# Half sums in the other order, and two of three images combined near the end: a convolution kernel on one Trainium2 core

## The chip, the cores and the metric

The kernel runs on one core of a Trainium2 chip. The metric is the device time of one execution in microseconds (us), as the median of several executions. Each execution has a state, fast or slow; on this one core slow means over 1.5% above the fastest run of the same kernel. Profiles are of one execution each. Engines are named as in the profile: PE is TensorE's matmul, PEld its weight load, DVE VectorE, ACT ScalarE, POOL GpSimd, SP SyncE. "Step i" is the loop's turn that convolves image i.

## The reference

160 images of 128 channels and 32 x 32 pixels are group-normalised (32 groups of 4 channels), convolved 3 x 3 with weights that are first quantised in two stages, and added to themselves. Five weight sets take the images in turn.

```python
# cut: helper functions, the setup of the inputs
s1 = (beta - alpha) / 3.0;  v1 = s1 * floor(U / s1)          # beta, alpha: max and min of U
s2 = s1 / 5.0;              v2 = s2 * floor((U - v1) / s2)
w = (v1 + v2).reshape(OUT_CH * N, IN_CH, 3, 3)
act = conv_general_dilated(gn(x) as (32, 640, 32, 32), w, padding 1, feature_group_count=5)
return x + act
```

## The kernel before

The arithmetic that the argument needs: rows are convolved in pairs, so that each image needs two *half sums* m1 and m2 in PSUM (128 x 512 float32, one bank each), from which the accumulators of the even and odd rows start: m1 + m2 and m1 - m2. Every operand is split into a high and a low float16 part. A *plain* image multiplies its high part directly; a *combined* image (the odd ones from image 7 on) has row combinations `v` formed by DVE before the split, which saves PE some products and costs DVE more work.

```python
LOAD_LEAD = 20
...
self.xpool = pool("x", 12)          # pairs of images
self.zpool = pool("z", 3)
self.parts = pool("parts", 5)
self.rows = pool("rows", 4)         # low parts
self.wide = pool("wide", 1)         # v of combined images
self.wide_parts = pool("wide_parts", 2)   # their high parts
self.evac = pool("evac", 2)         # copies of m2
self.sums = pool("sums", 4)
...
def combined(self, i):
    return self.STEADY <= i < self.imgs and i % 2 == 1
...
def sums_of_pairs(self, i):         # PE: the half sums of image i
    m = self.m[i] = self.banks(self.ps_m, "m", i)       # ONE tile of two banks, pool of 1
    both = self.both(i)
    for a, kind in enumerate((self.SUM, self.DIFF)):    # m1, then m2
        for col in self.COLS:
            for j, (_, st) in enumerate(both):
                self.product(m[:, a], i, kind, st[:, a], col, ...)
...
def leave(self, i):                 # ACT: copy m2 out of PSUM
    m2 = self.evac.tile(...)
    self.nc.scalar.copy(m2, self.m[i][:, 1])
    ...
def pairs(self, i, between=lambda: None):   # DVE: the two pair operations
    ...
    nc.vector.tensor_add(rows[:, :, 0], m[:, 0], m2)
    between()
    nc.vector.tensor_sub(rows[:, :, 1], m[:, 0], m2)
```

In step i PE first does the half sums of image i+1, then the rest of image i. DVE does, in this order, the low part of i+2, the pairs of i+1, and `v` of i+4 where that is combined. SP issues all large transfers in one order: at the end of step i the store of the pair of images that is finished, then the load of a later pair, and now and then a set of weights:

```python
self.store(i - 2)
while loaded * NB < min(self.imgs, i + self.LOAD_LEAD):
    self.load(loaded)
    loaded += 1
```

The sum of an image with its convolution goes ACT (`sum` from PSUM), POOL (a DMA that adds `sum` to the x tile), SP (store). Then the x tile can be loaded again.

## Time and profile before

| | before |
|---|---|
| time, median of 3 (range) | 1001.79 us (1001.14 to 1002.22) |
| profiled span | 1000.1 us |
| first half-sum product of image 145 | 900.79 us |
| start of the last product | 992.78 us |
| between the two: "the tail" | 91.99 us |

The two stretches have different limits: up to about 905 us ACT is nearly as busy as PE, afterwards ACT has room. So the table cuts the run at image 145, and the two marks are taken from the matmul starts. The lines of the page that bound the kernel are shown and read in the prediction.

The columns are start, duration, engine, line and operation.

### The profile page before, as it was taken

The numbers are of one execution on the slowest core, as the hardware profiler recorded it, in microseconds if no ns is written. First come the engines' busy times: TensorE is split into PE (matmuls) and PEld (weight loads), VectorE is DVE, ScalarE is ACT, GpSimd is POOL, SyncE is SP. The second block draws the span as 40 slices with busy tenths as digits, with TensorE's granted clock in tenths as the row PEclk, the third lists the DMA queues.
The fourth block names the chain that finished last, engine by engine and source line by source line (L and its number), as shares of the span: only waits on it lengthen the run. The fifth ranks groups of instructions, "written<-read, shape, count | busy, mean of one in ns | idle before, by whom it ended". The sixth has DMA issues, their size and how long they took to land.

```text
span 1000.1 us, 15977 instructions
## 1 busy us (share of the span) xinstructions
PE 962.5 (96%) x5935; PEld 575.1 (58%) x5935; DVE 895.6 (90%) x1237; ACT 913.2 (91%) x1243; POOL 405.3 (41%) x575
## 2 busy tenths in 40 slices
PE   1999999999999999999999999999999999999997
PEld 0445555565655565666655566666565666666554
DVE  7999999998999999989999998999999988888884
ACT  4879999999999999999999999999999999998560
POOL 3435473553425262524364443426353523233310
PEclk9999999999999999999999999999999999999999
DMA  9628989999999999999989999999999999988773
GB/s 357 247 89 229 257 221 279 269 268 267 272 273 269 266 258 273 288 274 269 264 243 288 270 265 278 277 273 249 266 272 270 279 262 275 274 230 219 177 179 141
DMA packets 67287, 254.42 MB, mean 254 GB/s; under 512 B 5248, under 2 KB 5248, under 8 KB 67200
## 3 DMA queue, kind: packets, MB, share of 16 engines
q1 hardware_dynamic: 45168, 173.09, 50.2%
q0 software_dynamic: 22032, 80.23, 41.4%
q8 instruction: 48, 0.79, 0.3%
q14 instruction: 39, 0.32, 0.1%
HBM read 89.19 MB, written 83.89 MB: 173 GB/s over the span
## 4 chain that ended last, share of the span: by engine, by line
PE 73%; DVE 10%; ACT 10%; issue 3%; POOL 3%; DMA 1%; SPq 0%; DVEq 0%; POOLq 0%
PE eo L613 25%; PE m L651 25%; PE eo L651 22%; ACT junk L199 2%; ACT vh L560 2%; ACT sum L735 1%; ACT m L709 1%; DVE eo L719 1%; DVE eo L721 1%; ACT z L510 1%; ACT junk L192 1%; DVE lo L573 1%; DVE vl L566 1%; DMA range<-in_L_conv_U_dram 1%; DVE ext L421 1%
## 5 line engine op out<-in xcount | busy, mean ns | idle before, releaser
L651 PEld LDWEIGHTS <-wt 128*128 128x128 f16 x4212 | 409.0, 98 | 241.3 <-DVE eo L721 12.9
L613 PE MATMUL eo<-hi,wt 128*128 128x496 f16 (+1 forms) x1476 | 352.5, 375 | 1.1 <-ACT wt L475 0.6
L748 POOL DMA_DIRECT2D xt<-sum x153 | 136.5, 895 | 419.4 <-ACT sum L735 403.5
L613 PEld LDWEIGHTS <-wt 128*128 128x128 f16 x1548 | 151.3, 99 | 147.4 <-ACT wt L475 1.8
L566 DVE SCALAR_TENSOR_TENSOR vl<-v,rstd,vh 128x2048 f16<-128x2048 f32 x77 | 180.8, 2348 | 4.2 <-ACT vh L560 4.2
L651 PE MATMUL m<-vh,wt 128*128 128x496 f16 (+1 forms) x462 | 175.7, 380 | 5.2 <-DVE eo L721 4.6
L719 DVE TENSOR_TENSOR eo<-m,m 128x512 f32<-128x512 f32 x157 | 109.0, 695 | 77.8 <-ACT m L709 77.8
L651 PE MATMUL eo<-vl,wt 128*128 128x256 f16 (+1 forms) x924 | 177.1, 273 | 0.0
L651 PE MATMUL eo<-vh,wt 128*128 128x256 f16 (+1 forms) x924 | 177.1, 273 | 0.0
L651 PE MATMUL m<-vl,wt 128*128 128x496 f16 (+1 forms) x462 | 175.4, 380 | 0.0
L199 ACT ACTIVATE junk<-xt,mv 128x1024 f16<-128x1024 f32 x152 | 174.0, 1145 | 0.2
L192 ACT ACTIVATE junk<-xt 128x1024 f16<-128x1024 f32 x152 | 160.6, 1057 | 14.7 <-DMA xt<-in_x_dram 11.6
L735 ACT ACTIVATE sum<-eo 128x1024 f32<-128x1024 f32 x153 | 154.1, 1007 | 13.7 <-PE eo L651 13.7
L560 ACT ACTIVATE vh<-v,rstd 128x2048 f16<-128x2048 f32 x77 | 155.0, 2013 | 1.8 <-POOL v L539 1.8
L651 PE MATMUL eo<-rows,wt 128*128 128x248 f16 (+1 forms) x960 | 144.3, 273 | 0.0
L651 PE MATMUL m<-rows,wt 128*128 128x496 f16 (+1 forms) x480 | 116.9, 380 | 0.5 <-DVE eo L721 0.5
L709 ACT COPY m<-m 128x512 f32<-128x512 f32 x157 | 91.3, 582 | 27.4 <-PE m L651 23.9
L721 DVE TENSOR_TENSOR eo<-m,m 128x512 f32<-128x512 f32 x157 | 108.4, 691 | 1.0
L510 ACT ACTIVATE z<-xt,shift,rstd 128x1024 f32<-128x1024 f32 x83 | 103.2, 1243 | 3.5 <-POOL shift L242 3.5
L573 DVE TENSOR_TENSOR lo<-z,hi 128x1024 f16<-128x1024 f32 x83 | 101.5, 1223 | 0.0
L518 ACT CAST hi<-z 128x1024 f16<-128x1024 f32 x83 | 86.8, 1046 | 2.6
L549 DVE TENSOR_TENSOR v<-xt 128x960 f32<-128x960 f32 x77 | 88.4, 1149 | 0.0
(111 smaller groups left out, 863.3 us busy)
## 6 DMA issues: line engine op xcount, KB each, us to landing
xt<-in_x_dram SPq DMA_DIRECT2D x78, 1024.0 KB, 9.0
out_dram<-xt SPq DMA_DIRECT2D x78, 1024.0 KB, 5.2
xt<-sum POOLq DMA_DIRECT2D x153, 512.0 KB, 6.9
range<-in_L_conv_U_dram SPq DMA_DIRECT2D x4, 576.0 KB, 7.9
u<-in_L_conv_U_dram SPq DMA_DIRECT2D x4, 576.0 KB, 11.8
xt<-in_x_dram SPq DMA_DIRECT2D x4, 512.0 KB, 10.6
out_dram<-xt SPq DMA_DIRECT2D x3, 512.0 KB, 2.7
u<-in_L_conv_U_dram SPq DMA_DIRECT2D x2, 288.0 KB, 3.0
```

Source lines behind the costliest of these rows:

```text
L192: self.nc.scalar.activation(junk, image, ACTF.Copy, scale=-1.0 / image.shape[1], accum_out=self.mv[:, j, 0:1],)
L199: self.nc.scalar.activation(junk, image, ACTF.Square, bias=self.mv[:, j, 0:1], accum_out=self.mv[:, j, 1:2],)
L510: nc.scalar.activation(z, self.image(i), ACTF.Identity, bias=st.shift[:, j : j + 1], scale=st.rstd[:, j : j + 1],)
L560: self.nc.scalar.mul(vh, self.v[i], st.rstd[:, j])
L566: self.nc.vector.scalar_tensor_tensor(vl, self.v[i], st.rstd[:, j], self.hi[i], ALU.mult, ALU.subtract)
L573: self.nc.vector.tensor_sub(lo[:, 1 : self.H + 1, :].rearrange("p h w -> p (h w)"), self.z.pop(i), self.hi[i].rearrange("p h w -> p (h w)"),)
L613: nc.tensor.matmul(target[:, h, r0 - h0 : r1 - h0, c0:c1], self.wts[n, col][:, k, :], tile[:, s0 : s0 + r1 - r0, c0 + dw : c1 + dw], start ...
L651: self.nc.tensor.matmul(target[:, :, c0:c1], self.wts[n, col][:, kind, :], source[:, :, c0 + dw : c1 + dw], start=start, stop=stop, skip_g ...
L719: nc.vector.tensor_add(rows[:, :, 0], m[:, 0], m2)
L721: nc.vector.tensor_sub(rows[:, :, 1], m[:, 0], m2)
L735: nc.scalar.mul(self.sum[i], eo, 0.5)
L748: self.nc.gpsimd.dma_start(self.image(i), self.sum.pop(i), accum_op=ALU.add)
```

## The change

The intent has two parts. With m2 multiplied first, ACT could copy it while PE still does m1, and PE could start the next m2 as soon as that copy is done. And near the end, where ACT has room, two of three images are combined rather than one of two, which takes work from PE; for that `v` and its high part need more tiles, which are taken from x, `sum` and the lead of the loads.

```diff
-    LOAD_LEAD = 20
+    LOAD_LEAD = 18
+    THIRDS = 146
...
-        self.xpool = pool("x", 12)
+        self.xpool = pool("x", 11)
-        self.wide = pool("wide", 1)
-        self.wide_parts = pool("wide_parts", 2)
+        self.wide = pool("wide", 2)
+        self.wide_parts = pool("wide_parts", 3)
-        self.sums = pool("sums", 4)
+        self.sums = pool("sums", 3)
...
+        self.pair = self.ps_m.tile([P, 2, self.H // 2, self.W], F32, tag="m", name="m")
...
-        return self.STEADY <= i < self.imgs and i % 2 == 1
+        if i < self.STEADY or i >= self.imgs:
+            return False
+        return i % 2 == 1 if i < self.THIRDS else i % 3 != 1
...
-        m = self.m[i] = self.banks(self.ps_m, "m", i)
+        m = self.pair
-        for a, kind in enumerate((self.SUM, self.DIFF)):
+        for a, kind in ((1, self.DIFF), (0, self.SUM)):
...
-        self.nc.scalar.copy(m2, self.m[i][:, 1])
+        self.nc.scalar.copy(m2, self.pair[:, 1])
```

(Cut: the same renaming in the warm-up, in the first images and in `pairs`.)

More of the change, by code (lines that the diff above doesn't have):

```diff
@@ L377, in __init__ @@
         self.steps = Steps(nc, keep)
-        self.chunks, self.z, self.hi, self.v, self.eo, self.m = {}, {}, {}, {}, {}, {}
+        self.pair = self.ps_m.tile([P, 2, self.H // 2, self.W], F32, tag="m", name="m")
+        self.chunks, self.z, self.hi, self.v, self.eo, self.m2 = {}, {}, {}, {}, {}, {}
         self.sum = {}
@@ L620, in taps, with bank_pair @@
                 )
-    def banks(self, pool, tag, i):
-        return pool.tile([self.P, 2, self.H // 2, self.W], F32, tag=tag, name=f"{tag}{i}")
+    def bank_pair(self, i):
+        return self.ps_eo.tile([self.P, 2, self.H // 2, self.W], F32, tag="eo", name=f"eo{i}")
     def warm_up(self, count):
         zeros = self.los[3].rearrange("p h w -> p (h w)")
-        if "warm" not in self.m:
-            self.m["warm"] = self.banks(self.ps_m, "m", "warm")
         for _ in range(count):
             self.nc.tensor.matmul(
-                self.m["warm"][:, 0].rearrange("p i w -> p (i w)"), zeros[:, :128],
+                self.pair[:, 0].rearrange("p i w -> p (i w)"), zeros[:, :128],
                 zeros[:, :512], start=True, stop=True,
@@ L639, in direct_hi @@
         if i not in self.eo:
-            self.eo[i] = self.banks(*((self.ps_eo, "eo") if i < 2 else (self.ps_m, "m")), i)
+            self.eo[i] = self.bank_pair(i) if i < 2 else self.pair
         self.taps(i, (self.hi[i], 0), col, self.eo[i], False)
@@ L708, in leave @@
         m2 = self.evac.tile([self.P, self.H // 2, self.W], F32, tag="m2", name=f"m2_{i}")
-        self.nc.scalar.copy(m2, self.m[i][:, 1])
-        self.m[i] = self.m[i], m2
+        self.nc.scalar.copy(m2, self.pair[:, 1])
+        self.m2[i] = m2
     def pairs(self, i, between=lambda: None):
         nc = self.nc
-        m, m2 = self.m.pop(i)
-        eo = self.eo[i] = self.banks(self.ps_eo, "eo", i)
+        m1, m2 = self.pair[:, 0], self.m2.pop(i)
+        eo = self.eo[i] = self.bank_pair(i)
         rows = eo.rearrange("p h (i a) w -> p (h i) a w", a=2)
-        nc.vector.tensor_add(rows[:, :, 0], m[:, 0], m2)
+        nc.vector.tensor_add(rows[:, :, 0], m1, m2)
         between()
-        nc.vector.tensor_sub(rows[:, :, 1], m[:, 0], m2)
+        nc.vector.tensor_sub(rows[:, :, 1], m1, m2)
     def by_hand(self, i):
```

## The prediction

> **What bounds the kernel now.** I read the page first, then busy time in windows, then the list of waits, then timelines of single engines near the end of the run, and last the built program, in which each wait names the instruction that ends it.
>
> ```profile
> PE 962.5 (96%) x5935; PEld 575.1 (58%) x5935; DVE 895.6 (90%) x1237; ACT 913.2 (91%) x1243; POOL 405.3 (41%) x575
> ...
> L719 DVE TENSOR_TENSOR eo<-m,m 128x512 f32<-128x512 f32 x157 | 109.0, 695 | 77.8 <-ACT m L709 77.8
> ```
>
> ```profile
> 600.00:700.00 100.00, 99.92 (x631) 60.81 (x629) 90.51 (x121) 98.74 (x136) 41.73 (x60) 1.00 0.98 269
> 940.00:960.00 20.00, 20.00 (x131) 12.58 (x129) 16.10 (x21) 12.63 (x13) 3.79 (x7) 1.00 0.75 196
> ```
>
> ```profile
> PE m L651 <- DVE eo L721: 4.6, 9, 1.2
> ```
>
> The windows' columns are the engines' busy us in the order of the page, then clock, DMA share and GB/s. PE is the bound, at full clock. But ACT is at 98.7% too until it stops measuring images (image 159 is measured while 145 is convolved, near 905 us), so in the middle it can't catch up what it loses. Afterwards ACT falls to 63% and DVE is at 80%. The waits view (100 to 900 us) shows PE waiting only 4.6 us for DVE; as ends of matmuls are modelled, I also took starts: over the run, 32 first half-sum products come late against the pitch, by 10.5 us together. That is all that a better order could ever win.
>
> Matmul starts give the size of each image: a product of 512 columns every 0.216 us, one of 256 every 0.109.
>
> ```profile
> 920.29 1.46 PE L651 MATMUL m<-rows,wt 128*128 128x512 f16 x6
> 921.59 0.38 PE L651 MATMUL eo<-vh,wt 128*128 128x256 f16 x2
> ...
> 924.35 0.38 PE L651 MATMUL m<-vh,wt 128*128 128x512 f16 x1
> ...
> 926.95 1.43 PE L613 MATMUL eo<-hi,wt 128*128 128x512 f16 x6
> ...
> 932.07 1.24 PE L651 MATMUL m<-rows,wt 128*128 128x512 f16 x5
> ```
>
> Half sums cost 1.30 us for a plain image (920.29 to 921.59) and 2.59 for a combined one (924.35 to 926.95); the rest 2.62 combined (24 x 0.109) and 5.13 plain (926.95 to 932.07). So 6.43 plain, 5.21 combined.
>
> **What the Trainium skill says.** "TensorE: Matmul & The Clock Gate", section Back-to-back issue gap, gives N/2.4 + 2.5 ns for a lone stream, 216 ns at 512, which the trace has; it also gives 131 ns for pairs of weight load and matmul, which this trace, made of such pairs, contradicts. "PSUM — Partial Sum Buffer", section PSUM bank collisions raise a hardware error, wants guards by bank and quadrant, "(by bank is the simple version)". m1 and m2 lie in two banks, so m2's could be overwritten while DVE reads m1: the reorder's idea is legal. Its section Engine vs sequencer instructions calls VectorE's queue strict FIFO; the timelines agree, and the third part below rests on it. "VectorE: DVE Perf Modes", section The TRN2 errata, has (N+151)/0.96 ns for an fp32 add, 691 at 512; the trace has 695. So no DVE operation here is about to be faster.
>
> **The change part by part.**
>
> *m2 first.* The intent: the copy of m2 by ACT starts half a group earlier, and the next group's first half waits for that copy alone. The built program says otherwise. In the changed kernel too, the copy waits for the last product of the whole group, and the first product of the next group (now m2's) waits for DVE's second pair operation (the last reader of m1). Semaphore values are the same as before in the steady part: the waits are kept for the tile of two banks, not for its halves. Effect: 0. For image 5, and for 151 and 157, the m2 half needs the third rows operation, which DVE does after the pairs: 0.3 us at 5, next to nothing later.
>
> *Two of three combined.* From 146 on, 146, 150, 152, 156, 158 become combined and 151, 157 plain: three more, 3 x (6.43 - 5.21) = 3.7 us less PE work. But the loop PE, ACT copy, DVE pairs, PE has to close in time. DVE's pieces stand here:
>
> ```profile
> 934.18 0.70 DVE L719 TENSOR_TENSOR eo<-m,m 128x512 f32<-128x512 f32 x1 [2.04 <-ACT m L709]
> 934.92 0.70 DVE L721 TENSOR_TENSOR eo<-m,m 128x512 f32<-128x512 f32 x1
> 935.53 1.15 DVE L549 TENSOR_TENSOR v<-xt 128x960 f32<-128x960 f32 x1
> 936.59 0.75 DVE L552 SCALAR_TENSOR_TENSOR v<-xt,twice 128x512 f32<-128x512 f32 x1
> 937.25 0.69 DVE L555 TENSOR_TENSOR v<-xt 128x512 f32<-128x512 f32 x1
> 937.86 1.22 DVE L573 TENSOR_TENSOR lo<-z,hi 128x1024 f16<-128x1024 f32 x1
> ...
> 941.59 2.34 DVE L566 SCALAR_TENSOR_TENSOR vl<-v,rstd,vh 128x2048 f16<-128x2048 f32 x1
> ```
>
> From starts: first pair operation 0.74 (0.94 with a rows operation between, 940.05 to 940.99), second 0.61 (its end 0.70), the combined rows v 2.33 (935.53 to 937.86), their low part vl 2.33. In the program, step i has DVE do the low part of i+2, the pairs of i+1, v of i+4. Call the steps of three a, b (combined), c (plain). In step a DVE does pairs of b, then v; in step b it does vl, then pairs of c. So between the end of b's half sums and the start of the product that needs c's pairs:
> - DVE's way: 0.20 to the copy, 0.61 to the first pair operation (both from the ACT and DVE timelines), 0.94 + 0.61 pairs of b, 2.33 v, 2.33 vl, 0.74 + 0.70 pairs of c, 0.06 to PE: 8.5.
> - PE's way: rest of a 2.62, half sums of c 1.30, rest of b 2.62: 6.5.
> PE waits 2.0 (2.1 where the third rows operation follows the pairs). This comes in steps 147, 150, 153 and 156: 8.3. Where the pattern starts, 145, 146 and 147 are combined in a row, and the same bookkeeping gives 0.7 more. Applied to the kernel before, it gives the pairs' starts at 2.11 and 4.06 us after the half sums' starts, where the trace has 2.12 and 4.06. In sum the part costs 9.0 - 3.7 = 5.3 us. Each engine's busy time would not show it: two combined and one plain are about 15.8 us of DVE work against 16.85 of PE; it is the order in the queue that does it.
>
> *Smaller pools.* A second v tile, a third vh tile are paid for by one x tile (12 to 11), one sum tile (4 to 3) and LOAD_LEAD 20 to 18. In the program each load of two images takes the place of the next one, two steps (11.8 us) later.
>
> ```profile
> xt<-in_x_dram SPq DMA_DIRECT2D x66, 1024.0 KB, 9.0
> ```
>
> ```profile
> 703.51 0.95 SPq L406 DMA_DIRECT2D xt<-in_x_dram  x1
> ```
>
> ```profile
> 713.31 1.06 ACT L192 ACTIVATE junk<-xt 128x1024 f16<-128x1024 f32 x1
> ```
>
> Before, from landing to the first read by ACT 14.6 us pass at the median, 10.0 at least. This load, issued at 703.5, landed 11.7 later at 715.2 and served the pair of images read at 725.2; in its place the changed kernel loads the pair read at 713.3, so ACT waits 1.9. Done for all 66 places, six come late: 0.7, 1.5 (a further 0.6 right behind it), 1.3, 1.9 (a further 0.8). The ones right behind are covered by the wait ahead of them; 5.4 remain. ACT cannot make it up, PE has 0.06 to 0.5 us of room per step: I take off 0.35 each and charge 4.0 us. Three sum tiles: between the landing of a sum's accumulation and the third next sum 1.8 us at least, 8.8 median: free. The second v tile takes away a wait of POOL for DVE (1.8 us in all) that holds nobody: 0.
>
> Sum: 1001.8 + 0 + 5.3 + 4.0, and 0.3 at image 5: 1011.4; I say 1010.5, since the late loads are few and shift with each run.
>
> **Rivals.**
> - *The reorder works.* If the chip's or the program's waits let PE run half a group ahead, up to 9 of the 10.5 us go, and the 2 us waits of the tail shrink by half a group (0.65): about 990 to 995 with the loads on time. Against it: the built waits, read directly.
> - *The tail gains its 3.7.* If DVE's order did not bind (80% busy speaks for slack), 998, or 1002 with late loads. Against it: strict order, and bookkeeping that fits the trace to 0.1 us.
> - *Loads are never late*, as landing times adapt: 1007. For it: the later issue meets the same traffic. Against it: the same loop of sum, accumulation, store, load that sets the issue stays.
> - *Loads late throughout*, since DMA shares are 0.95 to 1.0 and medians leave only 3 us: 1016 or more.
>
> **Range and chances.** The tail's part is firm to 1.5 us, the loads' to 4: 1003 to 1015 holds 8 in 10. Two per cent faster would be below 981.8, more than all idle time and saved work (14 us) could give: 0.01. Slower than 1021.8 needs loads late everywhere: 0.03. Within: 0.96.
>
> **What would show it.** In the changed profile: waits of PE for the second pair operation grow by about 9 us after 905 us, as four gaps near 2 us, each with DVE busy (v, vl, pairs) through it; the copy of m2 still starts 0.2 us after the whole group, 1.50 and 2.79 after its start; ACT waits for input DMA a handful of times between 400 and 750 us, with PE gaps behind. Wrong if the copy starts 0.65 to 1.3 us earlier, if the tail after 905 us is shorter than before, or if ACT never waits for a load.

## More of the kernel before

The chain that ended last, by engine:

```profile
PE 73%; DVE 10%; ACT 10%; issue 3%; POOL 3%; DMA 1%; SPq 0%; DVEq 0%; POOLq 0%
```

PE carries 73% of it, and DMA 1%: transfers hardly appear in it. And SP's own timeline, store and load of one step:

```profile
606.38 0.38 SPq L753 DMA_DIRECT2D out_dram<-xt  x1
606.93 0.62 SPq L406 DMA_DIRECT2D xt<-in_x_dram  x1
```

The load is issued 0.55 us behind the store: it has a free tile and need not wait for the store to land.

## The result, and the profile after

| | before | after |
|---|---|---|
| median of 4 (range) | 1002.0 us (1001.14 to 1004.57) | 1009.41 us (1006.98 to 1011.2) |
| profiled span | 1000.1 us | 1009.5 us |
| half sums of image 145 | 900.79 us | 905.52 us |
| tail | 91.99 us | 96.62 us |

The ratio is 1.0068, with a 95% interval of 1.004 to 1.0096. Ratios here and below are the mean time of one kernel's fast runs over that of the other's of the same rounds, so not quite the ratio of the medians. The changed kernel is slower by less than one per cent. The profiled execution is the slowest of its four (1011.2 us); its marks add up to more than the medians do: 4.73 us before image 145 and 4.63 us after it, 9.4 in all against 7.4 between the medians.

First the page after: busy times, the group of the first pair operation, and the windows 600 to 700 us and 940 to 960 us (columns as in the prediction).

```profile
PE 960.5 (95%) x5935; PEld 574.3 (57%) x5935; DVE 902.2 (89%) x1237; ACT 912.1 (90%) x1240; POOL 416.2 (41%) x581
...
L723 DVE TENSOR_TENSOR eo<-m,m 128x512 f32<-128x512 f32 x157 | 109.1, 695 | 80.2 <-ACT m L713 80.1
...
PE 55%; ACT 15%; DVE 11%; issue 6%; DMA 6%; POOL 6%; SPq 0%; POOLq 0%; ACTq 0%; DVEq 0%
```

```profile
600.00:700.00 100.00, 99.22 (x620) 59.71 (x618) 90.27 (x121) 97.16 (x133) 40.28 (x58) 1.00 1.00 273
940.00:960.00 20.00, 18.16 (x117) 11.19 (x116) 15.76 (x18) 11.25 (x11) 6.25 (x10) 1.00 0.63 159
```

PE's busy time falls by 2.0 us and DVE's rises by 6.6, as combined images should do it, but the span grows: PE stands idle more often, at the same granted clock (1.00 in both kernels' windows). The two windows say where: in the middle PE 99.22 us of 100 after 99.92, ACT 97.16 after 98.74; near the end PE 18.16 of 20 after 20.00, with DVE and ACT less busy than PE there. In the chain that ended last PE falls from 73% to 55%, and DMA rises from 1% to 6%. Two causes, then. PE's waits, first from 100 to 905 us, then from 905 us on (us in total, times, longest):

```profile
PE m L655 <- DVE eo L725: 7.5, 13, 1.2
...
PE m L655 <- DVE eo L725: 7.3, 5, 1.8
```

Before, the first stretch had 4.6 us and the second no such line. Here is one of the waits of the second stretch: PE, then DVE through the gap, then ACT's copy. In brackets is the engine's idle time and what ended it.

```profile
946.81 0.38 PE L655 MATMUL eo<-vl,wt 128*128 128x248 f16 x2
949.03 0.39 PE L655 MATMUL m<-vh,wt 128*128 128x512 f16 x1 [1.84 <-DVE eo L725]
...
942.95 1.15 DVE L555 TENSOR_TENSOR v<-xt 128x960 f32<-128x960 f32 x1
944.02 0.74 DVE L558 SCALAR_TENSOR_TENSOR v<-xt,twice 128x512 f32<-128x512 f32 x1
944.69 0.68 DVE L561 TENSOR_TENSOR v<-xt 128x512 f32<-128x512 f32 x1
945.29 2.35 DVE L572 SCALAR_TENSOR_TENSOR vl<-v,rstd,vh 128x2048 f16<-128x2048 f32 x1
947.55 0.69 DVE L723 TENSOR_TENSOR eo<-m,m 128x512 f32<-128x512 f32 x1
948.28 0.70 DVE L725 TENSOR_TENSOR eo<-m,m 128x512 f32<-128x512 f32 x1
...
944.60 0.59 ACT L713 COPY m<-m 128x512 f32<-128x512 f32 x1 [0.29 <-PE m L655]
```

The copy is long done when DVE gets to the pairs: m2 was copied from 944.60 on, and DVE is at `v`, `vl` and only then at the pairs, without a break from 942.95 on. The product of the next half sums waits for the second pair operation, which ends at 948.98. By starts, the four such gaps are 1.86, 2.01, 1.89 and 2.01 us over the pitch, the usual spacing of starts. A fifth, of 0.39 us at 924.22, comes where the pattern begins.

In the middle, ACT's waits from 100 to 900 us, and two of them in its timeline:

```profile
ACT junk L192 <- DMA xt<-in_x_dram: 5.1, 5, 1.6
...
681.21 1.06 ACT L192 ACTIVATE junk<-xt 128x1024 f16<-128x1024 f32 x1 [1.49 <-DMA xt<-in_x_dram]
718.18 1.06 ACT L192 ACTIVATE junk<-xt 128x1024 f16<-128x1024 f32 x1 [1.56 <-DMA xt<-in_x_dram]
```

The same view before has no wait for an x transfer at all. From the landing of a load to ACT's first read of it, 14.6 us passed at the median before, and 3.0 after, 0.1 at least.

### The profile page after: what moved, and what is told of

The parts are those of the page before. It is cut to its first block, busy times and chain, and to the rows that moved or that the text cites. A ratio compares the mean times of both kernels' runs of the same rounds, so it can differ in the third digit from the quotient of the medians.

```text
span 1009.5 us, 15999 instructions
## 1 busy us (share of the span) xinstructions
PE 960.5 (95%) x5935; PEld 574.3 (57%) x5935; DVE 902.2 (89%) x1237; ACT 912.1 (90%) x1240; POOL 416.2 (41%) x581
## 4 chain that ended last, share of the span: by engine, by line
PE 55%; ACT 15%; DVE 11%; issue 6%; DMA 6%; POOL 6%; SPq 0%; POOLq 0%; ACTq 0%; DVEq 0%
PE m L655 19%; PE eo L619 19%; PE eo L655 15%; ACT junk L199 3%; DMA xt<-in_x_dram 3%; ACT vh L566 3%; DMA xt<-sum 2%; ACT m L713 2%; ACT sum L739 2%; DVE eo L723 2%; DVE eo L725 2%; ACT z L513 2%; DVE vl L572 1%; POOL rstd L235 1%; ACT junk L192 1%
## 5 line engine op out<-in xcount | busy, mean ns | idle before, releaser
L619 PE MATMUL eo<-hi,wt 128*128 128x496 f16 (+3 forms) x1422 | 339.7, 375 | 1.1 <-ACT wt L478 0.6
L655 PE MATMUL m<-vh,wt 128*128 128x496 f16 (+1 forms) x480 | 182.7, 381 | 15.2 <-DVE eo L725 14.6
L572 DVE SCALAR_TENSOR_TENSOR vl<-v,rstd,vh 128x2048 f16<-128x2048 f32 x80 | 187.9, 2349 | 4.0 <-ACT vh L566 4.0
L655 PE MATMUL eo<-vh,wt 128*128 128x248 f16 (+1 forms) x960 | 184.0, 273 | 0.0
L655 PE MATMUL eo<-vl,wt 128*128 128x248 f16 (+1 forms) x960 | 184.0, 273 | 0.0
L655 PE MATMUL m<-vl,wt 128*128 128x496 f16 (+1 forms) x480 | 182.3, 380 | 0.0
L566 ACT ACTIVATE vh<-v,rstd 128x2048 f16<-128x2048 f32 x80 | 161.0, 2013 | 3.0 <-POOL v L545 2.0
L655 PE MATMUL eo<-rows,wt 128*128 128x256 f16 (+1 forms) x924 | 139.0, 273 | 0.0
L655 PE MATMUL m<-rows,wt 128*128 128x496 f16 (+1 forms) x462 | 112.5, 380 | 1.0 <-DVE rows L596 0.8
L513 ACT ACTIVATE z<-xt,shift,rstd 128x1024 f32<-128x1024 f32 x80 | 99.5, 1244 | 4.0 <-POOL shift L242 4.0
```

Source lines behind the costliest of these rows:

```text
L513: nc.scalar.activation(z, self.image(i), ACTF.Identity, bias=st.shift[:, j : j + 1], scale=st.rstd[:, j : j + 1],)
L566: self.nc.scalar.mul(vh, self.v[i], st.rstd[:, j])
L572: self.nc.vector.scalar_tensor_tensor(vl, self.v[i], st.rstd[:, j], self.hi[i], ALU.mult, ALU.subtract)
L619: nc.tensor.matmul(target[:, h, r0 - h0 : r1 - h0, c0:c1], self.wts[n, col][:, k, :], tile[:, s0 : s0 + r1 - r0, c0 + dw : c1 + dw], start ...
L655: self.nc.tensor.matmul(target[:, :, c0:c1], self.wts[n, col][:, kind, :], source[:, :, c0 + dw : c1 + dw], start=start, stop=stop, skip_g ...
```

## The experiments

Twelve kernels ran. The theory has three parts: the new order does nothing, since m1 and m2 lie in one tile and waits are kept for tiles; the combined images lose in DVE's queue what they save on PE; and the smaller pools with the shorter lead make loads late. The rivals: the order itself costs or gains; the tail loses for another reason than DVE's order; the pools cost through `sum` or `v` tiles rather than loads. The median of the kernel before beside these runs was 1000.86 us, 1001.79, 1001.4 and 1002.35, so kernels are compared by their ratios.

### The order alone

The kernel before with its own pools and images, but m2 first and one lasting pair tile: only those lines of the diff above that bring in `self.pair` and the order of m1 and m2.

> Kernel before with the half sums multiplied m2 first and one lasting pair tile, everything else as before (no thirds, old pools). Theory (the built waits keep the whole pair together): same time as before, 1002 within 1.5 us; ACT's copy of m2 still starts 1.50 us after the start of a plain image's half sums and 2.79 at the earliest after a combined one's; PE waits for the second pair operation about 10 us by starts. Rival (the reorder works by itself): 993 to 997, copies 0.65 to 1.3 us earlier. Rival (it costs): over 1004.

Measured: 1002.04 us (1000.5 to 1002.66), ratio 1.0004 [0.9991, 1.0018]. Tail 91.99 us, as before; late first half-sum products over the run 33 with 10.72 us together, against 32 with 10.45. The new order is worth nothing in the way that it is built.

### The pools without the combined images

The changed kernel with `THIRDS = 160` in place of 146, so that no image is combined that wasn't before.

> Changed kernel with every second image combined to the end (no thirds), its smaller x and sum pools and its load lead of 18 kept. Theory (late loads cost about 4 us in the middle): 1006 (1004 to 1008), ACT waits 4 to 6 us for input DMA between 100 and 900 us, no gap over 0.6 us on PE after 905 us. Rival (pools cost nothing, all of the loss is in the tail): 1002. Rival (the third sum tile binds): ACT waits for the accumulation DMA before its sums.

Measured: 1005.03 us (1003.48 to 1005.96), ratio 1.0039 [1.0025, 1.0052]; tail 91.99 us again; ACT waits for x transfers 4.7 us in 4 places. So the pools with the lead cost about 3.9 us, all before image 145, and the 4.63 us of the tail are the combined images'.

### The low part made cheap, on purpose wrong

If the work that stands ahead of the pairs in DVE's queue sets the tail, making one long operation short must close the gaps, though all other waits and the number of instructions stay. From image 146 on the low part of a combined image is a copy of its high part. The result is wrong (relative error 0.032).

```diff
+        if i >= self.THIRDS:
+            self.nc.vector.tensor_copy(vl, self.hi[i])
+        else:
             self.nc.vector.scalar_tensor_tensor(
                 vl, self.v[i], st.rstd[:, j], self.hi[i], ALU.mult, ALU.subtract
             )
```

> Wrong result on purpose: from image 146 on the low part of a combined image is a plain 16-bit copy of its high part, an operation of about 0.7 us in place of 2.33, on the same tiles, in the same place of DVE's queue, with the same waits. Theory (the gap is the sum of DVE's operations behind the pairs, 8.5 against 6.5 us): gaps fall from 2.0 to 0.3 to 0.5 us, the tail from the half sums of 145 on takes 91 us against 96.6 in the changed kernel and 92.0 before; 1003 to 1005 in all. Rival (input, POOL or ACT sets the gaps): they stay near 2 us, 1008 to 1010.

Measured: 1002.95 us (999.35 to 1006.36), ratio 1.0009 [0.9992, 1.0027]; tail 89.99 us. DVE at the same place of the sequence as shown above, and PE's waits from 905 us on:

```profile
944.63 0.69 DVE L573 COPY vl<-vh 128x2048 f16<-128x2048 f16 x1
945.24 0.69 DVE L726 TENSOR_TENSOR eo<-m,m 128x512 f32<-128x512 f32 x1
...
PE m L658 <- DVE eo L728: 0.6, 3, 0.2
```

With 0.69 in place of 2.35 us ahead of the pairs, PE's wait falls from 7.3 to 0.6 us, and the tail is 2.0 us shorter than before and 6.6 shorter than after. The work ahead of the pairs in DVE's queue is what turned the saving into a loss. (Expected were 91 us, so the size of the gain came out larger than I had it.) This run shortens that work; none moves `vl` behind the pairs, so what another order would save isn't measured. That DVE's load as a whole isn't the cause is shown below: with two tiles the same operations stand in the same order, and the gaps of 2 us are gone.

### The lead alone

The kernel before with `LOAD_LEAD = 18` and nothing else: all 12 x tiles, all 4 `sum` tiles.

> Kernel before with one number changed: LOAD_LEAD 18 in place of 20 (still 12 x tiles, 4 sum tiles, old order, no thirds). Theory (the loads' two steps later are the whole cost of the pools): the time of pools_alone, 1004 to 1006, ACT waits 4 to 6 us for input DMA. Rival (the 11th x tile or the third sum tile is needed for the loss): 1001 to 1002.

Measured: 1004.66 us (1003.32 to 1005.71), ratio 1.0024 [1.0012, 1.0037].

```profile
ACT junk L192 <- DMA xt<-in_x_dram: 6.4, 9, 1.6
```

The shorter lead alone brings the late loads and most of the pools' cost (0.24% of 0.39%; the intervals overlap). What is left, if anything, the other tiles would owe. The profiled executions show no such rest: from the half sums of image 20 to those of image 145 lead_alone takes 742.31 us, pools_alone 741.58, the changed kernel 742.37, and the kernel before 738.66.

### The lead given back without the tile: a miss

If the late loads come from the lead, the lead of 20 should take them away again. The changed kernel with `LOAD_LEAD = 20`, but its 11 x tiles.

> Changed kernel with LOAD_LEAD 20 again but 11 x tiles: each load is asked for two steps (11.8 us) earlier and then waits about 5 us for the store just ahead of it to land, as it takes that tile. Theory: no wait of ACT for input between 100 and 900 us, so only the tail's loss stays: 1005.5 (1004.5 to 1007); four PE gaps near 2 us after 905 us as before. Rival (the load blocks the queue and stores and loads pile up): 1009 or more.

Measured: 1022.46 us in the five fast runs (1017.04 to 1026.73; a sixth, of 1034.16, was slow), ratio 1.0205 [1.0179, 1.0232]. Against the changed kernel that is 1.4% slower (1.0205 over 1.0068), not faster. SP's timeline, its waits from 100 to 900 us, and one gap of PE:

```profile
637.49 0.37 SPq L409 DMA_DIRECT2D xt<-in_x_dram  x1
637.91 1.16 SPq L402 DMA_DIRECT2D u<-in_L_conv_U_dram  x1
639.19 0.72 SPq L757 DMA_DIRECT2D out_dram<-xt  x1
651.86 0.37 SPq L409 DMA_DIRECT2D xt<-in_x_dram  x1
...
SPq L409 <- DMA out_dram<-xt: 486.0, 66, 13.7
...
649.71 2.74 PE L655 MATMUL m<-rows,wt 128*128 128x512 f16 x6 [9.83 <-DVE eo L725]
```

The tile that a load wants is now the one that the store issued just ahead of it is still reading. So SP stands at the load until the store has landed: 12.7 us between the store at 639.19 and the load at 651.86, where before it was 0.55 us. And SP issues in order: what comes behind that load, the next store or a set of weights, stands too. DVE waits 11.45 us until 646.7 for weights that were asked for late in this way (at 637.91, behind a load that had itself stood for a store), and PE stands 10 us behind it. The gap costs more than its length: the granted clock was 0.50 from 646 to 650 us and 0.65 from 650 to 655, and the next half sums of a plain image took 2.53 us (649.71 to 652.24) in place of 1.30. With 12 tiles a load takes a tile that was stored two steps earlier, with 11 the one just being stored. I had foreseen that wait, but at 5 us and without cost; the blocked queue was my rival. Stores took 7.4 us to land at the median here, up to 14.4, after 5.3 before: now a store is often issued 0.5 us behind a load, and the next load waits until it has landed.

### The weights asked for earlier: two more misses

To take the weights out of that queue, each set from the third on is asked for two steps earlier, ahead of the store (cut: the old request, which falls away for these sets):

```diff
+            ahead_n, ahead_b = self.place(i + 2)
+            if ahead_b == 0 and ahead_n + 1 < N_SETS:
+                self.load_set(ahead_n + 1)
```

> lead_back, whose loss was one PE gap of 10 us where a set of weights came late behind an x load that waited for its tile in the same queue; here each set of weights from the third on is asked for two steps earlier. Theory: that gap goes, ACT waits under 2 us for x, and only the tail's loss of 4.7 us stays: 1005 to 1007. Rival (the blocked queue costs in other places too): 1010 or more.

Measured: 1018.96 us in the four fast runs (1015.21 to 1026.41; two slow ones, 1030.83 and 1032.99), ratio 1.0182 [1.015, 1.0214]; its profile fell in the slow state, so I read no size from it. The 10 us gap at the weights is gone, but ACT waits for x transfers in 20 places. The same in the kernel with two one-bank tiles (next but one):

> two_tiles_lead_back with the weights asked for two steps earlier. Theory: no gap of 12.8 us, x loads in time, thirds' gain of 2.8 us in the tail: 991 to 993, the fastest of all. Rival (x loads on 11 tiles stay late): 994 to 996 as all_two_tiles; rival (queue blocked elsewhere): over 1000.

Measured: 1022.39 us (1018.42 to 1027.33), ratio 1.0211 [1.0189, 1.0234]; ACT waits 30.4 us in 26 places for x transfers. So the weights were one victim of the queue, not its cause. Asking for them earlier even made this kernel slower than without (ratio 1.0121 [1.0079, 1.0162] further down); why, no run shows. One link of the loop (sum, accumulation, store, load of the same tile) can be seen in the trace: stores take 11.2 us to land at the median, so that one load follows the other every 12.2 us, where before it was 11.8 and two images take 11.8. Whether that link alone passes the delay on stays open; that the loop goes with the twelfth tile is shown by the last experiment.

### m1 and m2 as two tiles

If one tile of two banks is what keeps the new order from working, two tiles of one bank must let it work. To the order alone:

```diff
-        self.pair = self.ps_m.tile([P, 2, self.H // 2, self.W], F32, tag="m", name="m")
+        self.half = [
+            self.ps_m.tile([P, self.H // 2, self.W], F32, tag=f"m{h}", name=f"m{h}")
+            for h in range(2)
+        ]
```

(`m[:, a]` becomes `m[a]` in the places that use it; image 2, which is convolved straight into the pair, adds its residual in two halves.)

> As order_alone, but m1 and m2 are two tiles of one bank each, so that the built program waits for each half by itself: m2's products wait for ACT's copy, m1's for the second pair operation, the copy waits for m2's products alone. Theory (the intent of the reorder is right and only the shared tile undid it): most of the 10 us of late half sums go, 993 to 997; copies start 1.11 us after a plain image's half sums at the earliest (end of the sum before it) and 1.50 after a combined one's. Rival (ACT at 98.7% is the real bound in the middle): 999 to 1002, the PE gaps move elsewhere.

Measured: 994.96 us (993.75 to 995.78), ratio 0.9935 [0.9922, 0.9949]. PE's wait for DVE falls to

```profile
PE m L660 <- DVE eo L730: 0.6, 1, 0.6
```

from 100 to 905 us, and late first products to 3 with 2.45 us. ACT's copy now starts at the earliest 0.85 us after a plain image's first product and 1.50 after a combined one's; in the kernels with one tile, before, after and order_alone, it is 1.50 and 2.79. The tail is 91.99 us as ever: PE had no gap there before, so nothing was to be won in it.

Is it the tiles or the order? The same kernel with `for a, kind in ((0, self.SUM), (1, self.DIFF))`, so m1 first:

> order_two_tiles with the old order, m1 first, in two tiles; pools and images combined as before. Theory (order and tiles are both needed): m1's products come first and wait for the second pair operation as before, so about 10 us of late products stay: 1000 to 1002. Rival (the tiles alone do it): 994 to 996.

Measured: 1002.29 us (1000.11 to 1003.68), ratio 1.0004 [0.9992, 1.0016], with PE's wait for DVE at 4.8 us in 9 places. Neither does anything alone. It needs both: with m1 first, the first product must wait for DVE's second pair operation anyhow, as that reads m1; with m2 first in one tile it waits for it needlessly.

### The whole change with two tiles

> The whole change with m1 and m2 in two tiles. Theory: in the tail the 2 us gaps shrink to 0 to 0.6 us and the tail after 905 us becomes about 2.4 us shorter than before's, against 4.7 longer in the changed kernel; in the middle the half sums' gaps go but loads still come late: 992 to 998 in all. Rival (the tail's gaps come from something else than the order of DVE behind the pairs, such as input or POOL): gaps of 2 us stay, 1000 or more.

Measured: 995.59 us (994.73 to 996.38), ratio 0.9945 [0.9931, 0.9958]; tail 89.17 us, 2.8 shorter than before. Now the combined images win most of what they were meant to, for the pairs have to be ready half a group later: by starts 0.8 us of gaps are left in the tail, 0.27 us the longest, most of them at m1's first product, which waits for the second pair operation. But ACT waits 9.5 us in 7 places for x transfers, and what the tail gains the loads take back: it is no faster than the order with two tiles alone.

The lead given back to this kernel, with 11 tiles:

> all_two_tiles with LOAD_LEAD 20 on 11 x tiles. Theory: the late loads go (9.5 us of ACT's waiting there, about 2.6 us of the time), the thirds' gain stays: 991 to 993, under both kernels and under order_two_tiles (995). Rival (ACT is the bound in the middle, its waits just move): 994 to 996.

Measured: 1010.25 us (1008.8 to 1023.58), ratio 1.0121 [1.0079, 1.0162]. The same miss, and the same view: SP waits 508.4 us in 65 places at loads for the store ahead of them, and DVE once 13.6 us for weights.

### Twelve x tiles again

The whole change with two tiles, 12 x tiles and the lead of 20. The room comes from elsewhere:

```diff
-    LOAD_LEAD = 18
+    LOAD_LEAD = 20
-        self.xpool = pool("x", 11)
-        self.zpool = pool("z", 3)
-        self.parts = pool("parts", 5)
+        self.xpool = pool("x", 12)
+        self.zpool = pool("z", 2)
+        self.parts = pool("parts", 4)
-        ident = self.const.tile([P, P], F32, tag="ident", name="ident")
+        ident = self.qpool.tile([P, P], F32, tag="half", name="ident")
```

> The whole change with the pair as two one-bank tiles and with all twelve x tiles and the loads two steps early again; the room comes from one z tile (3 to 2), one parts tile (5 to 4) and the identity matrix's own buffer, so the three sum tiles of the changed kernel stay. If the late loads are what keeps the whole change with two tiles (995.59 us) from showing its tail gain over the order with two tiles (994.96), then the middle runs as in that kernel and the tail gives its 2.8 us: 991.5 to 993.5, with no wait of the Activation engine for an x transfer of more than 1.5 us in the middle. The rival: the missing z tile delays the start, or the third sum tile lets copies run where they disturb, so that the time stays at 994.5 or above although the tail is 89.2 us long.

Measured: 992.19 us (991.91 to 992.48, 4 runs), ratio 0.9902 [0.9885, 0.9918], correct. Half sums of image 145 start at 893.65 us (897.35 with 11 tiles and the lead of 18), the tail is 89.24 us; no wait of ACT for an x transfer is listed from 100 to 900 us. The window of the middle, and the place of the sequence in the tail where the changed kernel had its gap (PE, DVE, ACT):

```profile
600.00:700.00 100.00, 100.00 (x623) 60.41 (x622) 91.06 (x124) 99.06 (x136) 40.67 (x57) 1.00 1.01 277
...
933.12 0.38 PE L660 MATMUL eo<-vl,wt 128*128 128x248 f16 x2
933.34 0.38 PE L660 MATMUL m<-vh,wt 128*128 128x512 f16 x1
...
933.33 0.69 DVE L728 TENSOR_TENSOR eo<-m,m 128x512 f32<-128x512 f32 x1
...
930.54 0.58 ACT L718 COPY m<-m 128x512 f32<-128x512 f32 x1
```

PE starts the next m2 at 933.34, one pitch after its last product, while DVE has only just begun with the pairs at 933.33: it needs only the copy that began at 930.54, done two us earlier. The copy itself starts 1.12 us after its group's first product at 929.42, before the six of the group are through at 930.71. This is the version that beats both kernels: the one before by 1.0%, and the changed one by 1.6% (0.9902 over 1.0068, not timed side by side). It also settles the miss above: 20 is a good lead where the tile that it takes has been stored two steps ago. (This kernel also has one z tile and one `hi` tile fewer; its middle, image 20 to image 145, takes 733.89 us, that of the order with two tiles 733.68, so they cost nothing to be seen.)

## Why the prediction was right

The time was predicted at 1010.5 us and measured at 1009.41, and every step can be held against a number. That the sum came so near is in part luck: its terms made 1011.4, 0.9 was taken off by judgement, and the four runs of the changed kernel lie 4.2 us apart.

- *m2 first is worth 0.* Right: order_alone 1.0004, and in the changed kernel the second pair operation is what ends PE's waits. The cause given, waits kept for the tile, was only read from the built program; order_alone and the two runs with two tiles, one in either order, show it. The sign named for it held too: ACT's copy starts no earlier than before (1.50 and 2.79 us).
- *The tail: +9.0 of waits, -3.7 of work, +5.3 in sum.* Measured +4.63. The four gaps of 2.0 to 2.1 came as 1.86, 2.01, 1.89 and 2.01, 7.77 of 8.3, and the first three combined images gave 0.39 in place of 0.7. Without these 8.16 us of gaps the tail is 88.46 us, so the work saved is 3.5 of 3.7. The mechanism is shown by cheap_low, and by the rows above in which DVE has no break. The kernel with two tiles gains 2.8 and not 3.5, as it keeps 0.8 us of gaps.
- *The pools: 4.0 from late loads.* Between image 20 and image 145 the changed kernel lost 3.71 us (742.37 us between the two marks after, 738.66 before). The six late loads of the list came as five, 0.4 to 1.6 us, 5.1 in sum, where 5.4 were left after covering; four of them lie between 455 and 719 us, as forecast, the fifth at 849. pools_alone has 0.39%, and lead_alone shows that the lead, not the tile count, brings most of it.
- *Image 5: 0.3.* By image 20 the profiled run was 1.0 us behind (163.15 against 162.14), 0.6 of it by image 5. Too small; order_alone shows 0.7 at image 20 and has all but 0.2 of it lost again by image 145, so I put no weight on it.
- *The rival "the reorder works", 990 to 995*, was wrong for this program and right for one with two tiles: order_two_tiles 994.96, and with the tail's waits gone too 992.19. Its size for the tail was too small: the waits of 2 us shrank to 0.3 at most, not by 0.65. *Loads late throughout, 1016 or more*: three of the four kernels with the lead of 20 on 11 tiles passed 1016, but from a queue that stood, not for the reason given there; in the two with the weights asked for earlier loads were late in 20 and 26 places, in lead_back in 4.
- What I had not foreseen is what one tile does to the lead: the prediction treats the x tile and the lead as one saving, which they are in the changed kernel, and doesn't ask what would follow if only one were given back.

## What to carry to other kernels

An order that should free one half of a buffer early does so, in programs built like this one, only where the halves are tiles of their own: read in the built program (each engine's instructions with the waits that the build put in) which instruction the first product waits for, and try tiles and order together, as each alone can be worth nothing. Work moved to an engine that is 80% busy can still cost more than it saves, if it stands in that engine's queue ahead of what the bound engine waits for; count from the queue's order, not from the busy share. And a prefetch distance and a number of buffers belong together: a load that takes the buffer of the store just ahead of it blocks its whole queue.

## What the Trainium skill lacked or had wrong

- "TensorE: Matmul & The Clock Gate", section Back-to-back issue gap, has 131 ns per matmul of 512 columns in a stream of weight loads and matmuls. Here, in a stream of 5935 such pairs, products of 512 columns start every 216 ns at the median, before and after, the figure that the section calls the isolated gap and says over-counts.
- "Perfetto Trace Analysis", section Optimizing Tensor Performance, advises that matmul groups rotate through different PSUM banks so that evacuation overlaps the next group. The advice lacks a condition, which is of the program's build and not of the chip: m1 and m2 were in two banks all along, and the overlap came only with a tile for each (0.9935 with, 1.0004 without).
- The same page's section Identifying the Most-Contended Engine ranks engines by occupancy (TensorE by other measures). From 940 to 960 us DVE was busy 15.76 us of 20, with room to spare, and set the end all the same, by what stood in its queue; making one operation of 2.35 us take 0.69 shortened the tail by 6.6 us. How such a loop can be counted from the order in a queue, before the change is made, is not in that section.
- The same page's section DMA Optimizations advises separate issuing engines for inputs and outputs, to allow more dynamic spread. It doesn't say there what sharing one can cost: here a load that waits for its tile holds back all transfers behind it on the issuing engine. With the lead of 20 on 11 tiles that was 486.0 us of such waits in 66 places, one PE gap of 10 us, and 1.4% of the time. Separate engines were not tried.
